# A ConvNeXt block and two Mamba layers in one kernel: convolution bands read with a sliding offset, six batches of convolution per stage, and a layer norm moved from VectorE to GpSimd

## The chip, the core and the metric

The kernel runs on one core of a Trainium2 chip. Its time is the device time of a whole execution in microseconds (us), shown as the median of several runs. A core has five engines that run their own instruction streams: TensorE (PE in the profile), VectorE (DVE), ScalarE (ACT), GpSimd (POOL) and SyncE (SP), which here issues nearly all DMAs.

## The reference, cut to what matters

Input is x of 32 x 96 x 56 x 56 in float32.

```python
# layer 0: ConvNeXt block
h = depthwise_conv7x7(x) + conv_b                  # padding 3, one 7x7 filter per channel
h = layernorm_over_channels(h) * ln_g + ln_b
x = (gelu(h @ w1 + b1) @ w2 + b2) * layer_scale + x
# layer 1: two Mamba blocks over the 3136 pixels as a sequence, then a fusion
for i in range(2):
    h = layernorm_over_channels(seq) * ln_g[i] + ln_b[i]
    xs, z = split(h @ in_w[i])                      # 2 x 192
    xc = silu(causal_conv4(xs));  dt, Bm, Cm = split(xc @ xproj_w[i])
    delta = softplus(dt @ dt_w[i] + dt_b[i])
    state = scan(exp(delta * A), delta * Bm * xc)   # 192 channels x 16 states
    y = sum_over_states(state * Cm) + Dp * xc
    seq = seq + (y * silu(z)) @ out_w[i]
out = batchnorm(fus_w @ concat(seq, relu(mean(x) @ gp_w)) + fus_b) + x
```

## The kernel before

**Prologue.** The depthwise convolution is done on TensorE, two channels at a time (48 pairs). The 112 rows of a pair's image (2 x 56) lie on the partitions. For each of the 7 column shifts dw, a 112 x 112 band matrix holds the 7 filter rows on its diagonals, and a matmul of `band[:, dw, :]` with the padded image shifted by dw adds into PSUM. `conv_pair` (L157 to L184) does this for the first `b0 = 12` batches: it builds the band in SBUF by seven `copy_predicated` operations on DVE (L165) with seven masks that GpSimd made, stores the band to DRAM (`band_d`, L170), runs 2 x 7 matmuls of 6 batches x 56 = 336 columns (L176), adds the bias on ACT (L180) and stores the result (`conv_d`, L184). Bands and padded images have three buffers each. A scheduler orders this part. Then the first block (layer 0 after the convolution) of batch 0 is done on its own: `block0`, whose reading of the convolution is `cv` (L408).

**Stages.** After that come 256 stages: for each batch and each quarter of its sequence (784 positions), one stage for each of the two Mamba layers. The order of all engines is written out by hand here: a stage has 24 steps (`NSTEP`; six groups j of 32 channels x four groups g of states), `run(n, slots)` emits every piece of other work whose slot is n, and a slot below 0 or above 23 lies in the stage before or after. A step is one scan on DVE (L959) over 785 elements. Its inputs:

- the decay, an exponential by ACT (`exps`, L905), into SBUF (`da`) or PSUM (`w`);
- the input term, u times B. For four of six j, PE spreads u over the states into PSUM (`spread`, L931, with some filler matmuls L917 ahead of it, `FILL`) and DVE multiplies by B (`times_b`, L887); for j = 2 and 5 (`POOLED`) GpSimd does it from a broadcast copy `us` (`pooled`, L941).

After every second scan GpSimd multiplies the states by C (L964), and PE adds them up into `y` (`add_up`, L1005). ACT copies the last states for the next quarter (`keep_state`, L973, `KS` steps after the scan). A state tile has 7 buffers.

Beside the scans, a stage holds these pieces:

- `prep` of the next stage: centring, squares and means of the layer norm on PE and ACT, `root` (L387, L388: ACT's Ln and Exp, in place in PSUM), then `norm`, two DVE multiplications of 96 x 392 (L611) into `hn`; projections (L625), silu, softplus, the product u = delta * xc on GpSimd (L707), and the loads of B, C, delta (`d4`) and `us`;
- `post` of the stage before: the output projection and its moves;
- in stages 2 to 249, `block0` of a half quarter (392 positions) of a later batch; its own norm on DVE is L435;
- in stages 2 to 193, `conv` of one pair for one group of `NB = 5` batches: it loads the band that the prologue stored (L542) and the image (L543), does 7 matmuls of 280 columns (L552), and stores `conv_d`.

**Final pass.** The statistics of the batch norm, then a pass over the output.

Of the kernel before, what the change touches and what calls it, by code (L numbers as in the profile page):

```python
# [34 lines left out]
F32 = mybir.dt.float32  # L35
I32 = mybir.dt.int32
AF = mybir.ActivationFunctionType
ALU = mybir.AluOpType
# [23 lines left out]
def convnext_mamba_kernel(  # L62
# [38 lines left out]
    NB = 5  # L101
    b0 = B - 4 * NB if B > 4 * NB else B
    groups = [(0, b0)] + [(b, b + NB) for b in range(b0, B, NB)]
# [4 lines left out]
    band_d = dram.tile([C // 2, 2 * H, 7 * 2 * H], F32, name="band_d")  # L108
# [12 lines left out]
    ones = cc.tile([R2, R2], F32, name="ones")  # L121
    nc.vector.memset(ones, 1.0)
    masks = []
    for dh in range(7):
        m = cc.tile([R2, R2], F32, name="m", tag="m", bufs=2)

        nc.gpsimd.affine_select(
            out=m, in_=ones, compare_op=ALU.is_equal, fill=0.0, base=3 - dh,
            pattern=[[-1, R2]], channel_multiplier=1,
        )  # L130
        nc.gpsimd.affine_select(
            out=m[:, 0:H], in_=m[:, 0:H], compare_op=ALU.is_ge, fill=0.0, base=H - 1,
            pattern=[[0, H]], channel_multiplier=-1,
        )
        nc.gpsimd.affine_select(
            out=m[:, H:R2], in_=m[:, H:R2], compare_op=ALU.is_ge, fill=0.0, base=-H,
            pattern=[[0, H]], channel_multiplier=1,
        )
        mi = cc.tile([R2, R2], I32, name=f"mi{dh}", tag=f"mi{dh}")
        nc.vector.tensor_copy(mi, m)  # L140
        masks.append(mi)
    cw = cc.tile([R2, C // 2, 49], F32, name="cw")
    wv = conv_w.rearrange("(p two) k -> two p k", two=2)
    bv = conv_b.rearrange("(p two) k -> two p k", two=2)
    for j in range(2):
        nc.sync.dma_start(cw[j * H : (j + 1) * H], wv[j].partition_broadcast(H))
        nc.sync.dma_start(
            cb[j * H : (j + 1) * H].unsqueeze(2), bv[j].partition_broadcast(H)
        )
    bands, xpads = [], []  # L150
    for i in range(3):
        t = cc.tile([R2, 7, R2], F32, name=f"band{i}", tag=f"band{i}")
        nc.gpsimd.memset(t, 0.0)
        bands.append(t)
        t = cc.tile([R2, b0, W + 6], F32, name=f"xpad{i}", tag=f"xpad{i}")
        nc.gpsimd.memset(t, 0.0)
        xpads.append(t)  # L157
    def conv_pair(p):
        xp, T = xpads[p % 3], bands[p % 3]
        nc.sync.dma_start(  # L160
            xp[:, :, 3 : 3 + W],
            x[0:b0, 2 * p : 2 * p + 2, :].rearrange("b c (h w) -> (c h) b w", w=W),
        )
        for dh in range(7):
            nc.vector.copy_predicated(  # L165
                T,
                masks[dh].unsqueeze(1).broadcast_to([R2, 7, R2]),
                cw[:, p, dh * 7 : (dh + 1) * 7].unsqueeze(2).broadcast_to([R2, 7, R2]),
            )
        nc.sync.dma_start(band_d[p], T.rearrange("p k n -> p (k n)"))  # L170
        ct = cx.tile([R2, b0 * W], F32, name="ct")
        for lo in range(0, b0, GB):
            n = min(GB, b0 - lo)
            ps = cps.tile([R2, GB * W], F32, name="ps")
            for dw in range(7):
                nc.tensor.matmul(  # L176
                    ps[:, 0 : n * W], T[:, dw, :], xp[:, lo : lo + n, dw : dw + W],
                    start=(dw == 0), stop=(dw == 6),
                )
            nc.scalar.activation(  # L180
                ct[:, lo * W : (lo + n) * W], ps[:, 0 : n * W], AF.Identity,
                bias=cb[:, p : p + 1],
            )
        nc.sync.dma_start(conv_d[0][p * R2 : (p + 1) * R2, :], ct)  # L184
# [161 lines left out]
    with ExitStack() as main:  # L346
# [12 lines left out]
        def tok(a):  # L359
            return slice(a * HC, (a + 1) * HC)  # L360
# [23 lines left out]
        def rsqrt(ps):  # L384

            rs = ps[0:C, 0:HC]
            nc.scalar.activation(rs, rs, AF.Ln, bias=eps_c[0:C])  # L387
            nc.scalar.activation(rs, rs, AF.Exp, scale=-0.5)  # L388
# [5 lines left out]

        batch_bias = {}
        batch_sums = {}

        def block0(b, c, s):
# [3 lines left out]
            def load():  # L402
                if k == 0:
                    batch_sums[b] = work([C, NCH * 2], "sums", 2)
                v["cv"] = work([C, ROWS, W], "cv", 1)
                g = 0 if b < b0 else 1 + (b - b0) // NB
                at = (b - groups[g][0]) * W
                nc.sync.dma_start(  # L408
                    v["cv"],
                    conv_d[g].rearrange("(c h) w -> c h w", h=H)[  # L410
                        :, k * ROWS : (k + 1) * ROWS, at : at + W
                    ],
                )
# [15 lines left out]
            def root():  # L429
                if pre and s == 0:  # L430
                    exp_ln_tables()
                rsqrt(v["ps"])

            def norm():
                nc.vector.tensor_tensor(hn0s[s][0:C], v["cv"], v["ps"][0:C, 0:HC], ALU.mult)  # L435
# [47 lines left out]
            def fuse():  # L483
# [12 lines left out]
                (-6, load), (2, load_x), (11.2, center), (11.9, square), (12.4, mean),  # L496
                (12.6, root), (14.1, True, norm), (15.6, up), (15.8, gelu), (17.3, down),
                (18, residual),
# [35 lines left out]
        nc.vector.memset(xpad, 0.0)  # L534

        def conv(g, p):
            lo, hi = groups[g]
            v = {}

            def load():  # L540
                v["band"] = wp.tile([R2, 7, R2], F32, name="band", tag="band", bufs=1)
                nc.sync.dma_start(v["band"].rearrange("p k n -> p (k n)"), band_d[p])  # L542
                nc.sync.dma_start(  # L543
                    xpad[:, :, 3 : 3 + W],
                    x[lo:hi, 2 * p : 2 * p + 2, :].rearrange("b c (h w) -> (c h) b w", w=W),
                )

            def tap(dw):
                def piece():
                    if dw == 0:  # L550
                        v["ps"] = psum(2)
                    nc.tensor.matmul(  # L552
                        v["ps"][0:R2, 0 : NB * W], v["band"][:, dw, :], xpad[:, :, dw : dw + W],
                        start=(dw == 0), stop=(dw == 6),
                    )

                return piece

            def store():
                t = wp.tile([R2, HC], F32, name="sq", tag="sq", bufs=3)[:, 0 : NB * W]  # L560
                nc.scalar.activation(
                    t, v["ps"][0:R2, 0 : NB * W], AF.Identity, bias=cb[:, p : p + 1]
                )
                nc.sync.dma_start(conv_d[g][p * R2 : (p + 1) * R2, :], t)

            at = (5.9, 6.1, 7.8, 8.6, 9.2, 9.6, 10.4)
            return [(-1, load), (10.5, store), *[(at[dw], tap(dw)) for dw in range(7)]]
# [3 lines left out]
        AHEAD = {(2, 0): 0, (2, 1): 4.4, (5, 0): 12.3, (5, 1): 16.9}  # L571
# [5 lines left out]
        def prep(S):  # L577
# [20 lines left out]
            def root():  # L598
                for a in range(2):
                    rsqrt(v["ps"][a])  # L600
# [5 lines left out]
            def norm(a):  # L606
                def piece():
                    hn = v["hn"] = hns[i]
                    if c == 0 and a == 0:
                        nc.vector.memset(hn[:, 0:3], 0.0)  # L610
                    nc.vector.tensor_tensor(  # L611
                        hn[0:C, 3 + a * HC : 3 + a * HC + HC], S.seq[:, tok(a)],
                        v["ps"][a][0:C, 0:HC], ALU.mult,
                    )

                return piece
# [113 lines left out]
            def load_d4(j):  # L730
# [10 lines left out]
                (-18, load), (-12.3, center), (-11.9, square), (-12.1, halo), (-11.6, mean),  # L741
                (-11.2, root), (-9, True, norm(0)), (-8.5, True, norm(1)),
            ]
            t = (-4.5, -4.4, -5.3, -4.8, -4, 0.2, 1.3, 2.3, 2.9, 3.4, 4)
            if S in (stages[2], stages[-1]):
# [3 lines left out]
                    (12, norm(0)), (12, norm(1)),  # L749
                ]  # L750
                t = (12, 12, 13, 13, 14, 14, 15, 16, 17, 18, 19)
            elif S is stages[3]:
# [3 lines left out]
                    (-3, root), (-2, norm(0)), (-2, norm(1)),  # L756
# [11 lines left out]
                (max(16.8, t[8] + 2.2), load_bc(1, 1)), (max(19.8, t[8] + 2.2), load_bc(0, 1)),  # L768
                (t[9], dt), (t[10], softplus),
                (max(14, t[10] + 1.5), product), (max(18.3, t[10] + 3.1), store_u(0)),  # L770
                (25.3, store_u(1)),
                (max(16.5, t[10] + 2), load_d4(0)), (max(21.9, t[10] + 3), load_d4(1)),
                (max(20.3, t[10] + 3.2), load_u(0)), (23, load_d4(2)),
                (26, load_d4(3)), (32.9, load_u(1)), (30, load_d4(4)), (34, load_d4(5)),
            ]

        def post(S):
# [55 lines left out]
            if i == 1:  # L833
                pieces += [(12.7, save), (17.2, stat(0)), (19, stat(1))]
# [8 lines left out]
        KS = 2  # L843
        FILL = {0: 4, 4: 12}
# [326 lines left out]
```

## Time and profile before

| | |
|---|---|
| median of 3 runs | 16063.91 us (16063.67 to 16070.08) |
| profiled execution | 16065.38 us, span 16063.7 us |
| mean granted TensorE clock | 0.931 |
| PE busy | 13868.6 us, 86% |
| DVE busy | 15341.8 us, 96% |
| ACT busy | 11941.9 us, 74% |
| POOL busy | 13950.6 us, 87% |
| DMA, mean rate | 147 GB/s |
| convolution of the prologue ends | 443 us |
| first and last product u (L707) | 541.49 us and 15635.07 us |

The span is the time from the first to the last instruction of the profiled execution; its own time is 1.7 us longer. Busy shares are averages over parts with different limits, so the prediction reads them by stretch. In a group of instructions, the first number after the bar is the busy time, the second the mean duration of one in ns, and behind the second bar stands the idle time of the engine just before them with what ended it. A row of L176, L552 or another fp32 matmul counts two records per matmul.

### The profile page before, as it was taken

How to read it: one execution, taken by the hardware profiler on the slowest of the kernel's cores; microseconds unless marked ns; L12 is line 12 of the kernel's file. 1: busy time of each engine (PE TensorE's matmuls, PEld its weight loads, DVE VectorE, ACT ScalarE, POOL GpSimd, SP SyncE). 2: the span in 40 equal slices, each digit the busy share in tenths (PEclk: the TensorE clock that was granted, in tenths of full speed). 3: DMA queues.
4: the chain of work that ended last, by engine and by line, in shares of the span. 5: the costliest groups of instructions: out<-in, count | busy, mean ns of one | idle time of the engine just before them, and what ended most of it. 6: DMA issues, size and time to landing. Idle time of an engine off the chain costs nothing. (4 is left out here: it accounts for less than half of the span.)

```text
span 16063.7 us, 215150 instructions
## 1 busy us (share of the span) xinstructions
PE 13868.6 (86%) x74840; PEld 5981.5 (37%) x74840; DVE 15341.8 (96%) x12358; ACT 11941.9 (74%) x23139; POOL 13950.6 (87%) x4446
## 2 busy tenths in 40 slices
PE   8888988888988888888898888889888888888870
PEld 5333333333333333333333333333333333333330
DVE  8699999999999999999999999999999999999993
ACT  1577777777777777777777777777777777777763
POOL 1599999999999999999999999999999999999980
PEclk9899999999999999999999999999999999999985
DMA  4344444444444444444444444444444444444438
GB/s 112 110 148 147 149 149 146 149 147 149 150 146 149 147 149 150 146 149 147 148 150 146 148 148 148 149 146 148 147 148 139 136 138 137 138 139 139 138 123 293
DMA packets 1307226, 2362.65 MB, mean 147 GB/s; under 512 B 495918, under 2 KB 697914, under 8 KB 1306136
## 3 DMA queue, kind: packets, MB, share of 16 engines
q1 hardware_dynamic: 1296808, 2308.46, 47.0%
q10 hardware_dynamic: 7168, 38.54, 0.6%
q8 instruction: 590, 9.67, 0.2%
q14 instruction: 500, 4.10, 0.1%
q0 software_dynamic: 2160, 1.88, 0.1%
HBM read 1945.97 MB, written 402.41 MB: 146 GB/s over the span
## 5 line engine op out<-in xcount | busy, mean ns | idle before, releaser
L964 POOL TENSOR_TENSOR h<-h,cp 128x1568 f32<-128x1568 f32 x3072 | 9968.7, 3249 | 1177.4 <-DVE h L959 974.4
L959 DVE TENSOR_TENSOR_SCAN h<-w,h 128x785 f32<-128x785 f32 (+1 forms) x3072 | 5293.9, 1769 | 122.9 <-ACT w L905 110.1
L959 DVE TENSOR_TENSOR_SCAN h<-da,w 128x785 f32<-128x785 f32 (+1 forms) x3072 | 5389.6, 1775 | 2.6 <-ACT da L905 2.6
L941 POOL TENSOR_TENSOR h<-us,bp 128x1570 f32<-128x1570 f32 x1024 | 3318.0, 3240 | 56.3 <-PE y L1005 29.8
L905 ACT ACTIVATE w<-d,A 128x784 f32<-128x784 f32 x3072 | 2819.1, 918 | 671.3 <-DVE h L959 587.7
L887 DVE TENSOR_TENSOR w<-w,bp 128x786 f32<-128x786 f32 x3072 | 2916.0, 980 | 146.4 <-PE w L931 24.7
L905 ACT ACTIVATE da<-d,A 128x784 f32<-128x784 f32 x3072 | 2876.5, 947 | 12.7 <-DMA d<-dd 11.9
L1005 PE MATMUL y<-h,ssum 128*32 128x392 f32 x24576 | 2460.1, 511 | 79.5 <-POOL h L964 79.2
L625 PE MATMUL ps<-hn,wx 97*64 97x392 f32 x12288 | 2204.2, 500 | 9.1 <-DVE hn L611 9.1
L931 PE MATMUL w<-u,sel 64*128 64x393 f32 x4096 | 998.0, 562 | 1328.2 <-DVE h L959 1233.2
L904 ACT COPY w<-st 128x1 f32<-128x1 f32 x2304 | 371.6, 161 | 1510.9 <-DVE h L959 1473.4
L625 PEld LDWEIGHTS ps<-hn,wx 97*64 97x64 f32 x12288 | 814.8, 136 | 1331.2 <-issue 1296.6
L1005 PEld LDWEIGHTS y<-h,ssum 128*32 128x32 f32 x24576 | 662.4, 111 | 1643.5 <-issue 1416.8
L552 PE MATMUL ps<-xpad,band 112*112 112x280 f32 x2688 | 1032.5, 509 | 259.3 <-ACT dl L695 259.3
L707 POOL TENSOR_TENSOR u<-dl,xc 128x1176 f32<-128x1176 f32 x256 | 685.6, 2678 | 489.2 <-ACT dl L695 470.7
L917 PEld LDWEIGHTS y<-sel 128*128 128x128 f32 x8192 | 981.6, 193 | 253.2 <-issue 184.1
L917 PE MATMUL y<-sel 128*128 128x120 f32 x8192 | 1029.3, 279 | 14.6 <-DVE z L980 14.6
L887 DVE TENSOR_TENSOR h<-w,bp 128x786 f32<-128x786 f32 x1024 | 990.1, 967 | 0.0
L367 ACT ACT_TABLE_LOAD x759 | 973.8, 1283 | 14.2 <-PEq L1158 0.8
L931 PEld LDWEIGHTS w<-u,sel 64*128 64x128 f32 x4096 | 331.5, 190 | 1716.5 <-DVE h L959 980.6
L552 PEld LDWEIGHTS ps<-xpad,band 112*112 112x112 f32 x2688 | 490.2, 207 | 871.2 <-issue 450.6
L792 PE MATMUL ps<-z,ow 64*96 64x392 f32 x3072 | 797.1, 668 | 0.0
(158 smaller groups left out, 15917.6 us busy)
## 6 DMA issues: line engine op xcount, KB each, us to landing
d<-dd SPq DMA_DIRECT2D x1536, 392.0 KB, 3.6
bp<-bd SPq DMA_DIRECT2D x1024, 392.0 KB, 4.6
cp<-bd SPq DMA_DIRECT2D x1024, 392.0 KB, 6.0
us<-uu SPq DMA_DIRECT2D x512, 392.0 KB, 4.5
dd<-dl SPq DMA_DIRECT2D x512, 294.0 KB, 3.7
band<-band_d SPq DMA_DIRECT2D x192, 343.0 KB, 5.8
uu<-u SPq DMA_DIRECT2D x1024, 49.0 KB, 3.4
cv<-conv_d SPq DMA_DIRECT2D x256, 147.0 KB, 2.7
```

The costliest lines, as they stand in the source:

```text
L367: nc.scalar.preload_act_table_set("natural_log_exp_and_others")
L552: nc.tensor.matmul(v["ps"][0:R2, 0 : NB * W], v["band"][:, dw, :], xpad[:, :, dw : dw + W], start=(dw == 0), stop=(dw == 6),)
L625: nc.tensor.matmul(v["x", q][rows(a), 0:HC], weights[:, k, 64 * q : 64 * q + 64], v["hn"][:, o : o + HC], start=(k == 0), stop=(k == last),)
L792: nc.tensor.matmul(v["ps"][a][0:C, 0:HC], S.d["ow"][rows(a), q, :], S.z[rows(a), q, :], start=False, stop=(q == NQ - 1),)
L887: nc.vector.tensor_tensor(halves(S.pb[j, g]), halves(S.u4[j])[:, :, 0 : HC + 1], halves(S.bc[0, g // 2][:, g % 2, :]), ALU.mult,)
L905: nc.scalar.activation(e[:, 1 : 1 + CH], S.d4[j], AF.Exp, scale=S.d["A"][:, j, g : g + 1])
L917: nc.tensor.matmul(spare, sel[:, 0, :], sel.rearrange("p a b -> p (a b)")[:, 0 : 512 - HC], start=True, stop=True,)
L931: nc.tensor.matmul(u4[:, 512 * a : 512 * a + HC + 1], sel[rows(a), j % 2, :], S.u[rows(a), j // 2, a : a + HC + 1], start=True, stop=True,)
L941: nc.gpsimd.tensor_tensor(states(S, j, h)[:, :, 0 : 1 + CH], S.us[j].unsqueeze(1).broadcast_to([128, 2, 1 + CH]), S.bc[0, h][:, :, 0 : 1 + ...
L959: nc.vector.tensor_tensor_scan(h[:, g % 2, at], S.e.pop((j, g))[:, at], S.pb.pop((j, g), h[:, g % 2, :])[:, at], 1.0 if c else 0.0, ALU.mu ...
L964: nc.gpsimd.tensor_tensor(h[:, :, 0:CH], h[:, :, 1 : 1 + CH], S.bc[1, g // 2], ALU.mult)
L1005: nc.tensor.matmul(S.y[r0 : r0 + 32, 0:HC], ssum, hs[k][:, g, tok(a)], start=False, stop=(half == 1 and g == 1),)
```

## The change

It has four parts that were made together.

1. The band is no longer built on the partitions. Each channel's 49 weights are laid out once as 7 rows of 112 with the seven filter rows in the middle (`bw`), and stored in DRAM (`band_d`, 96 x 7 x 112). `load_band` reads, for partition k, 56 values from offset k on: the offset slides by row. The band that results gives the image rows in reverse order, so `cv` is read back row by row, 7 DMAs in place of 1. Only the two diagonal 56 x 56 blocks are written; the rest of the band tile is set to zero once.
2. `NB` is 6 in place of 5, so the prologue convolves 8 batches (`b0`) in place of 12, in two groups of 4, and each of the 192 stage parts convolves 6.
3. The norm of the next stage is one GpSimd multiplication of 96 x 784 in place in `hn`, where ACT now writes the reciprocal root; the two DVE multiplications are gone. (`ZP = 0` leaves the norm of `block0` on DVE.)
4. `KS` goes from 2 to 1, `FILL` has one filler matmul less in each of its two places, and many slots are moved.

```diff
-    NB = 5
+    NB = 6
-    band_d = dram.tile([C // 2, 2 * H, 7 * 2 * H], F32, name="band_d")
+    band_d = dram.tile([C, 7, 2 * H], F32, name="band_d")
...
+    cw = cc.tile([C, 49], F32, name="cw")
+    nc.sync.dma_start(cw, conv_w)
+    bw = cc.tile([C, 7, R2], F32, name="bw")
+    nc.vector.memset(bw, 0.0)
+    nc.vector.tensor_copy(bw[:, :, H - 4 : H + 3], cw.rearrange("p (h w) -> p w h", w=7))
+    nc.sync.dma_start(band_d, bw)
     for j in range(2):
-        nc.sync.dma_start(cw[j * H : (j + 1) * H], wv[j].partition_broadcast(H))
         nc.sync.dma_start(
             cb[j * H : (j + 1) * H].unsqueeze(2), bv[j].partition_broadcast(H)
         )
+    def load_band(T, p):
+        for j in range(2):
+            w = band_d[2 * p + j]
+            r = slice(j * H, (j + 1) * H)
+            nc.sync.dma_start(
+                T[r, :, r], bass.AP(w.tensor, w.offset, [[1, H], [R2, 7], [1, H]])
+            )
...
-        for dh in range(7):
-            nc.vector.copy_predicated(...)
-        nc.sync.dma_start(band_d[p], T.rearrange("p k n -> p (k n)"))
+        load_band(T, p)
...
-        def rsqrt(ps):
+        def rsqrt(ps, out):
-            nc.scalar.activation(rs, rs, AF.Exp, scale=-0.5)
+            nc.scalar.activation(out, ln, AF.Exp, scale=-0.5)
...
-                nc.sync.dma_start(
-                    v["cv"],
-                    conv_d[g].rearrange("(c h) w -> c h w", h=H)[
-                        :, k * ROWS : (k + 1) * ROWS, at : at + W
-                    ],
-                )
+                rows_d = conv_d[g].rearrange("(c h) w -> c h w", h=H)
+                for r in range(ROWS):
+                    nc.sync.dma_start(
+                        v["cv"][:, r, :], rows_d[:, H - 1 - k * ROWS - r, at : at + W]
+                    )
...
-                v["band"] = wp.tile([R2, 7, R2], F32, name="band", tag="band", bufs=1)
-                nc.sync.dma_start(v["band"].rearrange("p k n -> p (k n)"), band_d[p])
+                load_band(band, p)
...
-            at = (5.9, 6.1, 7.8, 8.6, 9.2, 9.6, 10.4)
-            return [(-1, load), (10.5, store), *[(at[dw], tap(dw)) for dw in range(7)]]
+            at = (5.7, 5.9, 6.6, 8.7, 8.8, 9.4, 10.2)
+            return [(-1, load), (10.3, store), *[(at[dw], tap(dw)) for dw in range(7)]]
...
-            def norm(a):
-                def piece():
-                    hn = v["hn"] = hns[i]
...
-                    nc.vector.tensor_tensor(
-                        hn[0:C, 3 + a * HC : 3 + a * HC + HC], S.seq[:, tok(a)],
-                        v["ps"][a][0:C, 0:HC], ALU.mult,
-                    )
+            def norm():
+                hn = v["hn"]
+                if c == 0:
+                    nc.gpsimd.memset(hn[:, 0:3], 0.0)
+                hn = hn[0:C, 3 : 3 + CH]
+                nc.gpsimd.tensor_tensor(hn, S.seq, hn, ALU.mult)
...
-                (-11.2, root), (-9, True, norm(0)), (-8.5, True, norm(1)),
+                (-11.2, root), (-10, norm),
-            t = (-4.5, -4.4, -5.3, -4.8, -4, 0.2, 1.3, 2.3, 2.9, 3.4, 4)
+            t = (-4.5, -4.4, -5.8, -4.8, -4.1, -1.2, 1.3, 2.3, 2.9, 3.4, 4)
...
-                (max(16.8, t[8] + 2.2), load_bc(1, 1)), (max(19.8, t[8] + 2.2), load_bc(0, 1)),
+                (max(17.6, t[8] + 2.2), load_bc(1, 1)), (max(17.5, t[8] + 2.2), load_bc(0, 1)),
-                (max(14, t[10] + 1.5), product), (max(18.3, t[10] + 3.1), store_u(0)),
-                (25.3, store_u(1)),
-                (max(16.5, t[10] + 2), load_d4(0)), (max(21.9, t[10] + 3), load_d4(1)),
-                (max(20.3, t[10] + 3.2), load_u(0)), (23, load_d4(2)),
-                (26, load_d4(3)), (32.9, load_u(1)), (30, load_d4(4)), (34, load_d4(5)),
+                (max(14, t[10] + 1.5), product), (max(17.1, t[10] + 3.1), store_u(0)),
+                (27.4, store_u(1)),
+                (max(15.3, t[10] + 2), load_d4(0)), (max(21.9, t[10] + 3), load_d4(1)),
+                (max(20.3, t[10] + 3.2), load_u(0)), (22.3, load_d4(2)),
+                (29.1, load_d4(3)), (34.2, load_u(1)), (29.9, load_d4(4)), (34, load_d4(5)),
...
-        KS = 2
-        FILL = {0: 4, 4: 12}
+        KS = 1
+        FILL = {0: 3, 4: 11}
```

More of the change, by code (lines that the diff above doesn't have):

```diff
@@ L98, in convnext_mamba_kernel @@
     const = ctx.enter_context(tc.tile_pool(name="const", bufs=1))
-    NB = 5
+    NB = 6
     b0 = B - 4 * NB if B > 4 * NB else B
-    groups = [(0, b0)] + [(b, b + NB) for b in range(b0, B, NB)]
+    groups = [(0, b0)] + [(b, min(b + NB, B)) for b in range(b0, B, NB)]
     conv_d = [
@@ L120, in convnext_mamba_kernel @@
     cps = first_conv.enter_context(tc.tile_pool(name="cp", bufs=6, space=PSUM))
-    ones = cc.tile([R2, R2], F32, name="ones")
-    nc.vector.memset(ones, 1.0)
-    masks = []
-    for dh in range(7):
[L125 to L129, printed above, removed]
-        )
-        nc.gpsimd.affine_select(
-            out=m[:, 0:H], in_=m[:, 0:H], compare_op=ALU.is_ge, fill=0.0, base=H - 1,
-            pattern=[[0, H]], channel_multiplier=-1,
-        )
[L135 to L143, printed above, removed]
+    cw = cc.tile([C, 49], F32, name="cw")
[4 more added lines that the diff above has]
+    nc.sync.dma_start(band_d, bw)
     bv = conv_b.rearrange("(p two) k -> two p k", two=2)
     for j in range(2):
-        nc.sync.dma_start(cw[j * H : (j + 1) * H], wv[j].partition_broadcast(H))
         nc.sync.dma_start(
@@ L152, in convnext_mamba_kernel @@
         t = cc.tile([R2, 7, R2], F32, name=f"band{i}", tag=f"band{i}")
-        nc.gpsimd.memset(t, 0.0)
+        nc.vector.memset(t, 0.0)
         bands.append(t)
@@ L163, in conv_pair @@
         )
[L164 to L169, printed above, removed]
-        nc.sync.dma_start(band_d[p], T.rearrange("p k n -> p (k n)"))
+        load_band(T, p)
         ct = cx.tile([R2, b0 * W], F32, name="ct")
@@ L382, in mean_of @@
             return ps
-        def rsqrt(ps):
-            rs = ps[0:C, 0:HC]
-            nc.scalar.activation(rs, rs, AF.Ln, bias=eps_c[0:C])
-            nc.scalar.activation(rs, rs, AF.Exp, scale=-0.5)
+        def rsqrt(ps, out):
+            ln = ps[0:C, 0:HC]
+            nc.scalar.activation(ln, ln, AF.Ln, bias=eps_c[0:C])
+            nc.scalar.activation(out, ln, AF.Exp, scale=-0.5)
+        ZP = 0
         batch_bias = {}
@@ L407, in load @@
                 at = (b - groups[g][0]) * W
-                nc.sync.dma_start(
-                    v["cv"],
-                    conv_d[g].rearrange("(c h) w -> c h w", h=H)[
-                        :, k * ROWS : (k + 1) * ROWS, at : at + W
-                    ],
-                )
+                rows_d = conv_d[g].rearrange("(c h) w -> c h w", h=H)
[3 more added lines that the diff above has]
+                    )
             def load_x():
@@ L431, in root @@
                     exp_ln_tables()
-                rsqrt(v["ps"])
+                v["rs"] = hn0s[s][0:C] if ZP else v["ps"][0:C, 0:HC]
+                rsqrt(v["ps"], v["rs"])
             def norm():
-                nc.vector.tensor_tensor(hn0s[s][0:C], v["cv"], v["ps"][0:C, 0:HC], ALU.mult)
+                eng = nc.gpsimd if ZP and not pre else nc.vector
+                eng.tensor_tensor(hn0s[s][0:C], v["cv"], v["rs"], ALU.mult)
             def up():
@@ L495, in block0 @@
             return last + [
-                (-6, load), (2, load_x), (11.2, center), (11.9, square), (12.4, mean),
-                (12.6, root), (14.1, True, norm), (15.6, up), (15.8, gelu), (17.3, down),
-                (18, residual),
+                (-6, load), (2, load_x), (11.2, center), (12, square), (12.4, mean),
+                (12.6, root), ((14.1, norm) if ZP else (14.1, True, norm)), (15, up), (15.2, gelu), (17.3, down),
+                (17.7, residual),
             ]
@@ L534, in convnext_mamba_kernel @@
         nc.vector.memset(xpad, 0.0)
+        band = wp.tile([R2, 7, R2], F32, name="band", tag="band", bufs=1)
+        nc.vector.memset(band, 0.0)
         def conv(g, p):
             lo, hi = groups[g]
+            nb = hi - lo
             v = {}
             def load():
-                v["band"] = wp.tile([R2, 7, R2], F32, name="band", tag="band", bufs=1)
-                nc.sync.dma_start(v["band"].rearrange("p k n -> p (k n)"), band_d[p])
+                load_band(band, p)
                 nc.sync.dma_start(
-                    xpad[:, :, 3 : 3 + W],
+                    xpad[:, 0:nb, 3 : 3 + W],
                     x[lo:hi, 2 * p : 2 * p + 2, :].rearrange("b c (h w) -> (c h) b w", w=W),
@@ L552, in piece @@
                     nc.tensor.matmul(
-                        v["ps"][0:R2, 0 : NB * W], v["band"][:, dw, :], xpad[:, :, dw : dw + W],
+                        v["ps"][0:R2, 0 : nb * W], band[:, dw, :], xpad[:, 0:nb, dw : dw + W],
                         start=(dw == 0), stop=(dw == 6),
@@ L559, in store @@
             def store():
-                t = wp.tile([R2, HC], F32, name="sq", tag="sq", bufs=3)[:, 0 : NB * W]
+                t = wp.tile([R2, HC], F32, name="sq", tag="sq", bufs=3)[:, 0 : nb * W]
                 nc.scalar.activation(
-                    t, v["ps"][0:R2, 0 : NB * W], AF.Identity, bias=cb[:, p : p + 1]
+                    t, v["ps"][0:R2, 0 : nb * W], AF.Identity, bias=cb[:, p : p + 1]
                 )
                 nc.sync.dma_start(conv_d[g][p * R2 : (p + 1) * R2, :], t)
-            at = (5.9, 6.1, 7.8, 8.6, 9.2, 9.6, 10.4)
-            return [(-1, load), (10.5, store), *[(at[dw], tap(dw)) for dw in range(7)]]
+            at = (5.7, 5.9, 6.6, 8.7, 8.8, 9.4, 10.2)
+            return [(-1, load), (10.3, store), *[(at[dw], tap(dw)) for dw in range(7)]]
         POOLED = (2, 5)
-        AHEAD = {(2, 0): 0, (2, 1): 4.4, (5, 0): 12.3, (5, 1): 16.9}
+        AHEAD = {(2, 0): 0.6, (2, 1): 4.4, (5, 0): 12.3, (5, 1): 16.9}
         seqs = {}
@@ L598, in root @@
             def root():
+                v["hn"] = hns[i]
                 for a in range(2):
-                    rsqrt(v["ps"][a])
+                    rsqrt(v["ps"][a], hns[i][0:C, 3 + a * HC : 3 + a * HC + HC])
             def halo():
@@ L604, in halo @@
                     nc.scalar.copy(hns[i][:, 0:3], hns[i][:, CH : CH + 3])
-            def norm(a):
-                def piece():
-                    hn = v["hn"] = hns[i]
-                    if c == 0 and a == 0:
-                        nc.vector.memset(hn[:, 0:3], 0.0)
-                    nc.vector.tensor_tensor(
-                        hn[0:C, 3 + a * HC : 3 + a * HC + HC], S.seq[:, tok(a)],
-                        v["ps"][a][0:C, 0:HC], ALU.mult,
-                    )
-                return piece
+            def norm():
[4 more added lines that the diff above has]
+                nc.gpsimd.tensor_tensor(hn, S.seq, hn, ALU.mult)
             def project(q, weights, taps_, first, last):
@@ L740, in prep @@
             start = [
-                (-18, load), (-12.3, center), (-11.9, square), (-12.1, halo), (-11.6, mean),
-                (-11.2, root), (-9, True, norm(0)), (-8.5, True, norm(1)),
+                (-18, load), (-12.3, center), (-12, square), (-12.1, halo), (-11.6, mean),
+                (-11.2, root), (-10, norm),
             ]
-            t = (-4.5, -4.4, -5.3, -4.8, -4, 0.2, 1.3, 2.3, 2.9, 3.4, 4)
+            t = (-4.5, -4.4, -5.8, -4.8, -4.1, -1.2, 1.3, 2.3, 2.9, 3.4, 4)
             if S in (stages[2], stages[-1]):
@@ L748, in prep @@
                     (10.3, center), (10.4, square), (10.5, halo), (10.9, mean), (11, root),
-                    (12, norm(0)), (12, norm(1)),
+                    (12, norm),
                 ]
@@ L755, in prep @@
                     (-18, load), (-4.5, center), (-4.4, square), (-4.3, halo), (-3.5, mean),
-                    (-3, root), (-2, norm(0)), (-2, norm(1)),
+                    (-3, root), (-2, norm),
                 ]
@@ L833, in post @@
             if i == 1:
-                pieces += [(12.7, save), (17.2, stat(0)), (19, stat(1))]
+                pieces += [(12.7, save), (17.2, stat(0)), (18.7, stat(1))]
             return pieces
```

## The prediction

> **What bounds the kernel now.** I read the busy times by stretch first, because this run has four parts: the prologue's convolution (0 to 443 us), the first block of batch 0 (to 541), 256 stages (to about 15,635) and the final pass. Columns: stretch, length, then busy us and instructions of PE, PEld, DVE, ACT, POOL, the granted clock, the DMA share, GB/s.
>
> ```profile
> 48.00:443.00 395.00, 390.59 (x1367) 238.50 (x1365) 336.72 (x355) 51.47 (x97) 20.76 (x36) 0.99 0.44 117
> 541.00:15635.00 15094.00, 13356.96 (x73024) 5688.09 (x73022) 14792.49 (x11815) 11692.61 (x22807) 13846.76 (x4333) 0.94 0.47 145
> ```
>
> In the first stretch PE is busy 390.6 of 395 us: TensorE binds, DVE (337) stands close behind. In the second DVE is busy 14,792 of 15,094 us, 98%; POOL has 92%. The costliest groups of the page, and two groups from the answer by line, say what fills them:
>
> ```profile
> L964 POOL TENSOR_TENSOR h<-h,cp 128x1568 f32<-128x1568 f32 x3072 | 9968.7, 3249 | 1177.4 <-DVE h L959 974.4
> ...
> L959 DVE TENSOR_TENSOR_SCAN h<-da,w 128x785 f32<-128x785 f32 (+1 forms) x3072 | 5389.6, 1775 | 2.6 <-ACT da L905 2.6
> ...
> L887 DVE TENSOR_TENSOR w<-w,bp 128x786 f32<-128x786 f32 x3072 | 2916.0, 980 | 146.4 <-PE w L931 24.7
> ```
>
> ```profile
> L165 DVE COPY_PREDICATED band<-mi,cw 112x784 f32<-112x784 int32 x336 | 346.9, 1037 | 32.1 <-PE ps L176 20.3 <-DMA cw<-in_conv_w 2.9
> ...
> L611 DVE TENSOR_TENSOR hn<-seq,ps 96x392 f32<-96x392 f32 x512 | 258.6, 544 | 36.4 <-ACT ps L388 36.4
> ```
>
> DVE's scans wait for almost nothing. The timeline of one stage shows the norm that moves (L611) between two scans, with no gap around it, and POOL at the same moment:
>
> ```profile
> 8049.76 1.78 DVE L959 TENSOR_TENSOR_SCAN h<-da,w 128x785 f32<-128x785 f32 x1
> 8051.46 0.53 DVE L435 TENSOR_TENSOR hz<-cv,ps 96x392 f32<-96x392 f32 x1
> 8051.91 1.77 DVE L959 TENSOR_TENSOR_SCAN h<-da,w 128x785 f32<-128x785 f32 x1
> 8053.61 1.00 DVE L611 TENSOR_TENSOR hn<-seq,ps 96x392 f32<-96x392 f32 x2
> 8054.54 1.77 DVE L959 TENSOR_TENSOR_SCAN h<-w,h 128x785 f32<-128x785 f32 x1
> ```
>
> ```profile
> 8051.62 3.24 POOL L964 TENSOR_TENSOR h<-h,cp 128x1568 f32<-128x1568 f32 x1 [1.05 <-DVE h L959]
> 8054.85 2.67 POOL L707 TENSOR_TENSOR u<-dl,xc 128x1176 f32<-128x1176 f32 x1
> 8057.48 3.26 POOL L964 TENSOR_TENSOR h<-h,cp 128x1568 f32<-128x1568 f32 x1
> ```
>
> L707 runs once a stage, so its starts give the period: of 243 stages from the fifth on, 145 take 58.0 to 58.7 us (a stage in which DVE never stops), 67 take 59.6 or more, the mean is 59.02. The 0.56 us above 58.46 is stalls. The waits between 4000 and 12000 us (135 stages) name them: 61.6 us of ACT's exponentials coming late, and POOL's reserve beside it, 512 us or 3.8 a stage.
>
> ```profile
> DVE h L959 <- ACT w L905: 61.6, 45, 2.0
> ```
>
> ```profile
> POOL h L964 <- DVE h L959: 512.2, 679, 2.2
> ```
>
> [...] the trace has 3249/1568 = 2.07. [...] L964 between 4000 and 12000 us took 3.22 to 3.31 us under a DVE that is 98% busy[...].
>
> **The change part by part.**
>
> *Norm off DVE.* The pair of L611 takes 0.93 us from start to next start (8053.61 to 8054.54). Out of a stage without gaps that is 58.46 to 57.53. In 254 stages: **-236 us**. In two stages (the third and the last), norm and projections follow at once; there it waits on POOL behind a 3.25 us product, about +4 each: **+8**.
>
> *Norm on POOL.* One operation of 784 elements: by rate 784 x 2.07 = 1.62 us; by the line through L964 and L707 (1.46 ns an element and 0.96 us fixed) 2.1. I take 1.8. POOL has 54.4 us of work a stage (12 x 3.25, 4 x 3.2, 2.63), so 56.2 against 57.5: covered by its wait for scans. It stands behind L707 and ahead of the product of scan 15. That product ends at about 8062.6 instead of 8060.7; PE's sums that read it came at 8004.78 + 58.4 = 8063.2 in the stage's rhythm. The next thing behind them on PE, the spread of u for the next stage, waits 1.34 us for DVE already. So nothing, with 0.5 to 1.9 us of cover. If the cover is gone, the spread is late next, then L887.
>
> *Exponentials into SBUF, keep_state one step earlier (KS), other slots.* ACT's write target changes, not its count. At the steps with the tightest exchange, the ACT exponential waits for the same scan that the earlier state copy needs; elsewhere ACT's lead shrinks by a step. Not shown before; between -0.56 (all stalls gone) and +0.6 us a stage; I take 0.
>
> *Conv of 6 batches in 192 stages.* Seven matmuls go from 280 to 336 columns; at 1.70 ns a column (0.57 us for 336 in the prologue) that is +0.67 us of PE a stage, less two filler matmuls (L917, about 0.28 together): +0.4. PE's idle time is 6.8 us a stage (15,094 less 13,357, over 255). Hidden; the next spread (wait 0.80) would be late if not.
>
> *Transfers of a stage.* SP issues 7 instead of 1 for cv and 2 instead of 1 for band; at 0.36 and 0.59 us each (SP timeline at 8007 to 8014) +2.8 us. The results are wanted some 17 steps, 40 us, later. Moved ahead of cv's issue are store_u(0), load_bc and load_d4(0); load_u(1) now stands behind load_d4(5), so us lands at about 32 us of the stage while POOL wants it at 31.5 and has until 36. The band becomes 784 runs of 224 bytes for 112 of 3136; cv, 672 such runs, lands in 2.7 us. DMA share is 47%. I take 0; bound 0 to +0.5.
>
> *Prologue.* The 336 L165 operations go, but PE bound. A pair takes 7.98 us (ACT's L180 two by two); 14 matmuls of 224 columns take 14 x 0.38 = 5.32. 48 pairs: **-128**. DMA per pair: 1680 short runs; 1344 of them landed in 4.4 us before. Three buffers give a band load about 10.6 us from release to need, for some 7 of issue and landing: hidden. At the start, SP's queue shows what delays the first matmul (47.8 us):
>
> ```profile
> 0.81 0.45 SPq L146 DMA_DIRECT2D cw<-in_conv_w  x1
> 1.31 2.13 SPq L147 DMA_DIRECT2D cb<-in_conv_b  x1
> 3.50 11.82 SPq L146 DMA_DIRECT2D cw<-in_conv_w  x1
> 15.36 10.17 SPq L147 DMA_DIRECT2D cb<-in_conv_b  x1
> 25.57 20.85 SPq L160 DMA_DIRECT2D xpad<-in_x  x3
> ```
>
> The broadcasts of cw go; two of cb stay (some 10 us each), then a band_d write and the first band load, each 3 to 4 us: first matmul at 31 (bounds 15 and 45): **-17**. The first block waits for 6 more issues in front of its first cv and some of its second: **+5**; its following norm on POOL **+1**.
>
> Sum: -236 + 8 - 128 - 17 + 5 + 1 = -367. The profiled execution took 16065.4 us, 1.5 above the median: 15,698, or **15,697** against the median.
>
> **The rivals.** (1) *The remaining ACT stalls go too*, because several ACT pieces get new slots: 254 x 0.56 = 142 less, 15,555. For it: 145 stages already run free. Against: the pieces that collide with the pooled scans (moves at 8.9 and 9.2) stay. (2) *The prologue becomes bound by band loads.* If a pair stays at 8 us, 128 are lost: 15,825. For it: each load now waits for a released buffer and stands in SP behind a ct store; against: 10.6 us of lead. (3) *POOL's lateness reaches DVE*, slower than before: norm puts POOL at 98% of DVE's period; once the product of scan 15, or a pooled product that waits for us, is over 1.9 us late, PE's sums hold back the next spread and DVE stands. At 2 us a stage it gives +508: 16,205. It decides from 367/254 = 1.44 us a stage. For it: covers of 0.5 to 1.9 us. Against: POOL needs to grow by 1.3 + 1.4 us a stage beyond my 1.8, a norm of 4.5. (4) *The change does not do what it says*: the built program's instruction order has L611's successor on POOL behind u, and none of it on DVE. Not likely.
>
> **How the numbers follow.** The likeliest case 0.60, rival 1 0.13, rival 2 0.11, rival 3 0.13, no net change by a mixture 0.03. The range goes from rival 1 less 15 us (an earlier first matmul), 15,540, to rival 2 plus 0.4 us of stalls a stage, 15,920. Faster 0.84, within 0.2% (32 us, about what a measurement of this kernel tells from no change) 0.03, slower 0.13.
>
> **What would show it.** Right: L176's successor at about 5.3 us a pair and the stages starting near 400; starts of the u product 57.5 apart in most stages; the norm at 1.6 to 2.1 us on POOL; POOL's wait for DVE down to about 1.3 us a stage. Wrong: waits of L887 for PE's spread, of PE's y for POOL, of h L941 for us, or of scans for ACT's w above 1 us a stage; PE waiting for band in the prologue.

## The result and the profile after

The changed kernel takes **16,568.8 us** (median of 4 runs, 16,568.4 to 16,586.5) against 16,064.5 before: a ratio of 1.032, 95% interval 1.030 to 1.033. It is 504 us slower; 367 us faster was forecast. The profiled execution is the highest of the four, 16,586.5 us, 18 above the median.

The starts of the product u on GpSimd (L707 before, L694 now) divide the difference between the two profiled executions, +521 us:

| part | before | after | difference |
|---|---|---|---|
| up to the first u | 541.5 | 410.3 | -131 |
| first to last u (255 periods) | 15,093.6 | 15,740.8 | +647 |
| after the last u | 428.6 | 433.7 | +5 |

So the prologue gave nearly what it was to give (139 us were forecast), and the stages lost 2.5 us each: the mean period is 61.6 us in stages with a convolution and 61.5 in those without, where it was 59.0. The profile of the same window as before, 541 to 15,635 us, in the same columns (the stages of the kernel after run from 410 to 16,151, so the whole window lies within them):

```profile
541.00:15635.00 15094.00, 13554.89 (x69472) 5577.47 (x69469) 14055.50 (x10808) 11268.96 (x22005) 13704.30 (x4469) 0.94 0.46 138
```

DVE, 98% busy before, is 93% busy; PE stands at 90% and POOL at 91%. By busy time alone no engine is full. What each waits for says more. In these answers, for 4000 to 12000 us or 130 stages, the numbers behind the colon are the us in total, the number of waits and the longest one:

```profile
PEld y L992 <- POOL h L951: 581.6, 437, 1.9
POOL h L928 <- DMA us<-uu: 488.3, 101, 5.7
...
ACT z L625 <- PE ps L612: 388.3, 390, 2.7
...
DVE h L946 <- ACT w L892: 304.7, 251, 2.5
...
DVE z L967 <- PE y L992: 171.6, 130, 1.6
...
POOL h L951 <- DVE h L946: 77.8, 260, 2.7
```

GpSimd's old reserve, waiting for DVE, is 0.6 us a stage (3.8 before). In its place stands a wait for the load of `us`: 101 stages name the DMA, 4.8 us each, and the 29 others name an instruction that ended near the same moment (626 us together over 130 stages, again 4.8 each). Work of 56.0 us (7,276 busy over 130), 4.8 and 0.6 make 61.4: **the period is GpSimd's**. One stage on GpSimd:

```profile
8116.62 6.54 POOL L951 TENSOR_TENSOR h<-h,cp 128x1568 f32<-128x1568 f32 x2 [0.20 <-DVE h L946]
8123.35 6.65 POOL L951 TENSOR_TENSOR h<-h,cp 128x1568 f32<-128x1568 f32 x2 [0.19 <-DVE h L946]
8134.39 3.23 POOL L928 TENSOR_TENSOR h<-us,bp 128x1570 f32<-128x1570 f32 x1 [4.38 <-DMA us<-uu]
8137.58 3.24 POOL L951 TENSOR_TENSOR h<-h,cp 128x1568 f32<-128x1568 f32 x1
8140.78 2.69 POOL L694 TENSOR_TENSOR u<-dl,xc 128x1176 f32<-128x1176 f32 x1
8143.43 1.84 POOL L603 TENSOR_TENSOR hn<-seq,hn 96x784 f32<-96x784 f32 x1
8145.23 3.25 POOL L951 TENSOR_TENSOR h<-h,cp 128x1568 f32<-128x1568 f32 x1
```

The gap of 4.38 us stands ahead of the pooled product of j = 5; from there on GpSimd runs without a pause into the next stage. The queue of SP at that time:

```profile
8115.04 9.85 SPq L721 DMA_DIRECT2D d<-dd  x3
8124.98 1.20 SPq L663 DMA_DIRECT2D bp<-bd  x2
8126.28 1.20 SPq L663 DMA_DIRECT2D cp<-bd  x2
8127.57 0.56 SPq L710 DMA_DIRECT2D us<-uu  x1
```

Slot 34.2 of one stage and slots 10 and 10.2 of the next are the same place, so load_u(1) is issued behind the sixth load of delta *and* the four broadcasts of B and C for the stage to come. us is issued at 8127.57 and arrives at about 8134.3, where GpSimd's wait ends, some 6.7 us later; in the kernel before this second load of us took 4.3 (median of 128), and it stood ahead of all five (8035.69 against 8041.77 to 8044.87).

How GpSimd's lateness reaches DVE is seen some 30 us earlier, behind the late pooled product of the stage before, in one line each of PE, ACT and DVE:

```profile
8100.46 1.51 PE L992 MATMUL y<-h,ssum 128*32 128x392 f32 x12 [1.09 <-POOL h L951]
```

```profile
8102.83 0.50 ACT L625 ACTIVATE z<-ps 128x392 f32<-128x392 f32 x1 [2.66 <-PE ps L612]
```

```profile
8107.11 1.79 DVE L946 TENSOR_TENSOR_SCAN h<-w,h 128x785 f32<-128x785 f32 x1 [1.70 <-ACT w L892]
```

PE's sums wait for GpSimd's product; the projection of z behind them on PE's queue is late; ACT waits for it with silu of z; the exponential behind that is late; DVE's scan waits, 2.3 us a stage in all (304.7 over 130). DVE's own product with y (L967) waits for the late sums directly, another 1.3.

### The profile page after: what moved, and what is told of

Read it like the earlier page. It is cut to its first block, busy times and chain, and to the rows that moved or that the text cites. A ratio compares the mean times of both kernels' runs of the same rounds, so it can differ in the third digit from the quotient of the medians.

```text
span 16584.8 us, 215686 instructions
## 1 busy us (share of the span) xinstructions
PE 14442.4 (87%) x73816; PEld 6060.2 (37%) x73816; DVE 14833.0 (89%) x11444; ACT 11923.2 (72%) x23139; POOL 14364.8 (87%) x4742
## 4 chain that ended last, share of the span: by engine, by line
POOL 27%; PE 20%; DVE 16%; DMA 12%; ACT 12%; issue 11%; SPq 2%; POOLq 0%; DVEq 0%; ACTq 0%
POOL h L951 20%; DVE h L946 13%; PE y L992 5%; DMA us<-uu 4%; PE ps L612 4%; POOL h L928 3%; PE ps L543 3%; DMA cp<-bd 3%; ACT da L892 3%; POOL hn L603 2%; DMA d<-dd 2%; ACT L354 2%; ACT w L892 2%; DVE w L874 2%; PE ps L163 2%
## 5 line engine op out<-in xcount | busy, mean ns | idle before, releaser
L992 PE MATMUL y<-h,ssum 128*32 128x392 f32 x24576 | 3035.5, 514 | 597.8 <-POOL h L951 594.4
L992 PEld LDWEIGHTS y<-h,ssum 128*32 128x32 f32 x24576 | 746.8, 110 | 2649.6 <-issue 1413.2
L543 PE MATMUL ps<-xpad,band 112*112 112x336 f32 x2688 | 1296.8, 612 | 237.2 <-ACT dl L682 237.2
L904 PEld LDWEIGHTS y<-sel 128*128 128x128 f32 x7168 | 863.6, 192 | 247.0 <-issue 182.4
L625 ACT ACTIVATE z<-ps 128x392 f32<-128x392 f32 x768 | 381.9, 497 | 753.5 <-PE ps L612 753.2
L674 PE MATMUL ps<-dbl,dtw 6*64 6x392 f32 x3072 | 733.5, 537 | 213.2 <-ACT dbl L647 213.2
L904 PE MATMUL y<-sel 128*128 128x120 f32 x7168 | 911.0, 279 | 7.7 <-DVE z L967 7.7
L543 PEld LDWEIGHTS ps<-xpad,band 112*112 112x112 f32 x2688 | 540.6, 227 | 964.0 <-issue 522.9
L603 POOL TENSOR_TENSOR hn<-seq,hn 96x784 f32<-96x784 f32 x256 | 471.9, 1843 | 323.7 <-ACT hn L375 317.0
```

What stands on the lines that cost most here:

```text
L543: nc.tensor.matmul(v["ps"][0:R2, 0 : nb * W], band[:, dw, :], xpad[:, 0:nb, dw : dw + W], start=(dw == 0), stop=(dw == 6),)
L603: nc.gpsimd.tensor_tensor(hn, S.seq, hn, ALU.mult)
L904: nc.tensor.matmul(spare, sel[:, 0, :], sel.rearrange("p a b -> p (a b)")[:, 0 : 512 - HC], start=True, stop=True,)
L992: nc.tensor.matmul(S.y[r0 : r0 + 32, 0:HC], ssum, hs[k][:, g, tok(a)], start=False, stop=(half == 1 and g == 1),)
```

## Experiments

Three theories were open. A: the place of load_u(1) in SP's queue makes GpSimd stand. B: GpSimd's norm alone does it. C: the short runs of the new loads slow all transfers. Kernels 1, 3 and 4 and the kernel after put the norm and that slot each in both places; kernel 2 moves the slot alone in the kernel before. Each ratio is against the kernel before, timed beside the kernel in question.

**1. After, with us early.**

```diff
-                (29.1, load_d4(3)), (34.2, load_u(1)), (29.9, load_d4(4)), (34, load_d4(5)),
+                (29.1, load_d4(3)), (32.9, load_u(1)), (29.9, load_d4(4)), (34, load_d4(5)),
```

> The kernel after, with one slot put back: the second load of us, load_u(1), at 32.9 as before in place of 34.2, so that SP issues it ahead of the sixth load of delta and of the loads of B and C. Theory A (the place of that load in SP's queue makes GpSimd stand, and with the norm GpSimd has no reserve left): GpSimd's wait for us goes from 3.6 us a stage to under 0.5, the period from 61.5 to 57.5 to 58.3 us, the time to 15,600 to 15,850. Theory B (the norm on GpSimd alone, through PE's sums that come late): a period of 61 us or more, 16,450 to 16,570. Theory C (short runs of the bands and seven-fold cv loads slow all transfers): us still lands 2 us or more late, 16,100 to 16,400.

Measured: 15,774.8 us, ratio 0.982 (0.981 to 0.984). The wait for us is gone from GpSimd's list; the fastest stages take 57.47 us, the mean is 58.4. SP issues us ahead of the sixth load of delta, 11 us before GpSimd wants it:

```profile
8124.44 0.51 SPq L710 DMA_DIRECT2D us<-uu  x1
8129.83 0.51 SPq L721 DMA_DIRECT2D d<-dd  x1
```

GpSimd at the same place:

```profile
8128.80 6.65 POOL L951 TENSOR_TENSOR h<-h,cp 128x1568 f32<-128x1568 f32 x2 [0.20 <-DVE h L946]
8135.40 3.24 POOL L928 TENSOR_TENSOR h<-us,bp 128x1570 f32<-128x1570 f32 x1
8139.68 3.23 POOL L951 TENSOR_TENSOR h<-h,cp 128x1568 f32<-128x1568 f32 x1 [1.03 <-DVE h L946]
8142.90 2.68 POOL L694 TENSOR_TENSOR u<-dl,xc 128x1176 f32<-128x1176 f32 x1
8145.53 1.85 POOL L603 TENSOR_TENSOR hn<-seq,hn 96x784 f32<-96x784 f32 x1
```

The pooled product starts without a gap, and GpSimd catches up with DVE ahead of u. One moved DMA issue is worth 794 us. Theory A holds; B and C fall as causes of the loss, since norm, band loads and cv loads are all still there.

**2. Before, with us late.**

```diff
-                (26, load_d4(3)), (32.9, load_u(1)), (30, load_d4(4)), (34, load_d4(5)),
+                (26, load_d4(3)), (34.2, load_u(1)), (30, load_d4(4)), (34, load_d4(5)),
```

> The kernel before, with the same slot alone moved the other way: load_u(1) at 34.2 in place of 32.9. Theory A: GpSimd waits some 3 to 4.5 us a stage for us; its reserve of 3.8 us takes most of that, so 16,050 to 16,300, likeliest 16,190, with a wait of h L941 for us above 2 us a stage. Theories B and C: nothing changes, within 0.2% of 16,064.

Measured: 16,357.8 us, ratio 1.019 (1.017 to 1.021). Direction and cause are as expected (the first row is GpSimd's wait, from the answer by waits); the size is above the range by 58 us. The wait ahead of that product is 4.9 us a stage (104 of 133 stages name the load), more than the 3 to 4.5 expected; GpSimd's wait for DVE, its reserve, falls from 3.8 us a stage to 0.9.

```profile
POOL h L941 <- DMA us<-uu: 510.3, 104, 6.3
POOL h L964 <- DVE h L959: 124.2, 280, 2.3
```

The slot alone makes the kernel before slower, with none of the other parts.

**3. After, with the norm on DVE and us late.** The norm is as in the kernel before:

```diff
-                    rsqrt(v["ps"][a], hns[i][0:C, 3 + a * HC : 3 + a * HC + HC])
+                    rsqrt(v["ps"][a], v["ps"][a][0:C, 0:HC])
...
-                (-11.2, root), (-10, norm),
+                (-11.2, root), (-9, True, norm(0)), (-8.5, True, norm(1)),
...
```

> The kernel after with the norm back on DVE as in the kernel before (root in PSUM, two multiplications on DVE between the same scans), load_u(1) left at 34.2. Theory A: GpSimd keeps its wait of 4.6 us for us but has 1.84 us less work, so the period is 59.4 to 59.9 us: 16,020 to 16,150. Theory B: the stages run as before, 59.0 us, and the shorter prologue remains: 15,930. Theory C: 60 us or more, above 16,170.

Measured: 16,166.4 us, ratio 1.007 (1.005 to 1.008), 16 us above A's range. GpSimd's wait for us is still there, 483 us in the 99 of 133 stages that name the load:

```profile
POOL h L932 <- DMA us<-uu: 483.1, 99, 6.5
```

**4. After, with both put back.** Experiment 3 with load_u(1) at 32.9.

> The kernel after with both put back: norm on DVE and load_u(1) at 32.9. What remains of the change is the band reading, the six batches per stage, KS, FILL and the other slots. Theories A and B: a period of 58.5 to 59.1 us, 15,800 to 15,950. Theory C: 59.5 us or more, above 16,050.

Measured: 15,974.9 us, ratio 0.995 (0.993 to 0.996), 25 us above the range. The fastest stages with a convolution take 58.41 us, as in the kernel before; the mean is 59.3.

The four together, medians in us:

| | us early (32.9) | us late (34.2) | cost of late |
|---|---|---|---|
| norm on DVE (3, 4) | 15,975 | 16,166 | +191 |
| norm on GpSimd (1, after) | 15,775 | 16,569 | +794 |
| gain of the move | -200 | +402 | |

The two parts do not simply add. The wait ahead of the pooled product is 4.8 to 4.9 us a stage in all three kernels with us late (after, 2 and 3), whether the norm is on GpSimd or not. What differs is GpSimd's work, 54.1 us a stage in experiment 3 and 56.0 in the kernel after. With us early the norm's move gains 200 us; with us late, 4.8 us of wait and 1.84 us of norm are in series on one engine, and the same move loses 402.

**5. us behind the load of delta, ahead of the broadcasts.**

```diff
-                (29.1, load_d4(3)), (34.2, load_u(1)), (29.9, load_d4(4)), (34, load_d4(5)),
+                (29.1, load_d4(3)), (29.9, load_d4(4)), (34, load_d4(5)), (34, load_u(1)),
```

> The kernel after with load_u(1) issued directly behind the sixth load of delta, but ahead of the four broadcasts of B and C that slot 34.2 puts it behind (slot 34, last of its entries). It tells apart what of the lateness of us comes from which neighbour. Theory A1 (the four broadcasts: 2.6 us of issue[...]): us lands at about 29 us of the stage, in time for GpSimd; wait for us under 1 us a stage, 15,750 to 15,900. Theory A2 (SP standing at the sixth load of delta until ACT frees its buffer): two thirds of the wait stay, above 2.5 us a stage, 16,150 to 16,450.

Measured: 15,779.5 us, ratio 0.982 (0.980 to 0.983), the same as experiment 1. SP's queue and GpSimd's wait:

```profile
8126.91 0.51 SPq L721 DMA_DIRECT2D d<-dd  x1
8127.53 0.54 SPq L710 DMA_DIRECT2D us<-uu  x1
8128.12 1.24 SPq L663 DMA_DIRECT2D bp<-bd  x2
```

```profile
POOL h L928 <- DMA us<-uu: 6.9, 16, 0.8
```

Here the pooled product started at 8132.48 without a gap, so us had landed within 5.0 us. From the issue of us to the moment when GpSimd is free for that product there are 11.6 us in experiment 1, 5.0 here and 2.4 in the kernel after (medians of 4000 to 12000 us). So the place behind the load of delta costs no time, but it takes 6.6 us of the lead and leaves just enough. The four broadcasts take 2.6 more for their issue, and us lands later behind them: in experiment 2, whose trace shows the landings, 7.0 us after its issue (median of 131) where the kernel before has 4.3. The broadcasts have to stand ahead of us for the wait to arise. Whether they would do it without the delay behind delta, and whether their issue or the slower landing alone would be enough, was not tried.

**6 to 8. The remaining stalls.** Experiment 1 has 0.9 us of stalls a stage above its fastest, 57.47, against 0.6 above 58.41 in the kernel before.

```diff
# 6: experiment 1 with
-        KS = 1
+        KS = 2
# 7: experiment 1 with the compute slots of before
-                (-6, load), (2, load_x), (11.2, center), (12, square), (12.4, mean),
-                (12.6, root), ((14.1, norm) if ZP else (14.1, True, norm)), (15, up), (15.2, gelu), (17.3, down),
-                (17.7, residual),
+                (-6, load), (2, load_x), (11.2, center), (11.9, square), (12.4, mean),
+                (12.6, root), ((14.1, norm) if ZP else (14.1, True, norm)), (15.6, up), (15.8, gelu), (17.3, down),
+                (18, residual),
...
-                (-18, load), (-12.3, center), (-12, square), (-12.1, halo), (-11.6, mean),
+                (-18, load), (-12.3, center), (-11.9, square), (-12.1, halo), (-11.6, mean),
...
-            t = (-4.5, -4.4, -5.8, -4.8, -4.1, -1.2, 1.3, 2.3, 2.9, 3.4, 4)
+            t = (-4.5, -4.4, -5.3, -4.8, -4, 0.2, 1.3, 2.3, 2.9, 3.4, 4)
...
-                pieces += [(12.7, save), (17.2, stat(0)), (18.7, stat(1))]
+                pieces += [(12.7, save), (17.2, stat(0)), (19, stat(1))]
# 8: 6 and 7 together
```

> The kernel after with load_u(1) at 32.9 and KS back at 2. In the first of these two alone the stages still stand 0.9 us each for ACT's exponentials, against 0.56 in the kernel before. If KS = 1 is what shortens ACT's lead: stalls back to 0.5 to 0.6 us a stage, 15,670 to 15,720. If not: within 0.2% of 15,775.

> The kernel after with load_u(1) at 32.9 and the slots of the compute pieces as in the kernel before (block0's square, up, gelu and residual; stat(1); the next stage's square and six projections); the loads, the conv taps and KS stay as changed. If these slots cause the additional ACT stalls: 15,670 to 15,720. If not: within 0.2% of 15,775; slower is possible, since the projections then stand closer behind GpSimd's norm.

> Both edits of the last two kernels together. If KS and the slots only work together, it is faster than either; if neither matters, 15,775 within 0.2%; if both do, 15,650 to 15,700.

Measured: 6 takes 15,763.6 us (ratio 0.981, 0.980 to 0.983), 7 takes **15,713.5** (0.978, 0.976 to 0.979), 8 takes 15,742.3 (0.980, 0.978 to 0.981). KS = 2 gains nothing that these runs can tell: 11 us less than experiment 1 with overlapping executions, and with the compute slots of before 29 us more than experiment 7, where the executions do not overlap but the intervals of the ratios do. The compute slots of before are worth 61 us. DVE waits less for ACT: 100.5 us in experiment 1, 40.8 in experiment 7, both in 4000 to 12000 us. In the whole run that wait falls by 104 us (183.4 to 79.7); a part is lost elsewhere, 12 us of it ahead of the first u (424 against 412).

```profile
DVE h L946 <- ACT w L892: 40.8, 50, 1.7
```

The stage's mean is 58.1 us, the stalls are 0.6. Experiment 7 beats both kernels, the kernel before by 356 us (16,069.5 beside it). Which of its slots does it was not tried apart.

## Why the prediction was wrong

**The step that failed is "Transfers of a stage".** It read the queue correctly up to one item: "load_u(1) now stands behind load_d4(5), so us lands at about 32 us of the stage while POOL wants it at 31.5 and has until 36". The stage above starts at 8096.6 (DVE's first product with B): GpSimd was ready at 33.4 us, and us arrived at 37.7. The four broadcasts (slots 10 and 10.2) that stand between load_d4(5) and slot 34.2 were not counted. Experiment 5 shows that with them behind us the place behind load_d4(5) costs nothing; with them ahead, "I take 0; bound 0 to +0.5" became a wait of 4.8 us a stage. "Has until 36" failed as well: it is 4.5 us of cover, where the prediction's own sum leaves GpSimd 1.3 (57.5 less 56.2).

**The cover was counted twice.** The norm adds 1.84 us to GpSimd's work and shortens DVE's stage (without gaps 58.41 us in experiment 4, 57.47 in experiment 1), so it uses up most of the reserve that was to cover a late us. With the norm on DVE, GpSimd's work and the wait for us make 54.1 + 4.8 = 58.9 us, near the 59.3 that a stage takes with us early (experiment 4). With the norm on GpSimd they make 56.0 + 4.8 = 60.8, against 58.4 (experiment 1). That is why the same slot costs 191 us with the norm on DVE and 794 with it on GpSimd.

**Rival 3 was the right mechanism**, "a pooled product that waits for us", with too small a price: 2 us a stage over the forecast, where it is 61.5 less 57.5, and less the stalls of the forecast, 3.4. Its way to DVE was half right: PE's sums are late, but the next spread hardly is (DVE waits 1.9 us for it in all 130 stages); the projection of z behind the sums and ACT's silu carry the delay, and DVE's own wait for y.

The other steps, by their own numbers:

- *Norm off DVE*: 57.53 us for a stage without gaps was worked out, 57.47 and 57.48 stand in experiments 1 and 7. The whole gain of the move, with us early, is 200 us against 228 (236 less 8).
- *Norm on POOL*: 1.8 us taken, 1.84 measured, between the rate of the trace (1.62) and the line through the two rows (2.1).
- *Prologue*: 5.32 us a pair taken; ACT's L167 shows 5.34 (median). First u 131 us earlier against 139 forecast (-128 - 17 + 5 + 1), because the first matmul came at 47.0 us, outside my 15 to 45 (47.8 before: 1 us gained, not 17); the pairs themselves gave 131, from 390 us between the first and last L180 to 259 between those of L167. I took some 10 us for each broadcast of cb, though my own lines show 2.13 and 10.17, and left the image load behind them out. The two of cb, 10.8 us of SP, and the first image, 22.9 more, kept the band's store back until 35:

```profile
1.20 10.83 SPq L129 DMA_DIRECT2D cb<-in_conv_b  x2
12.07 22.87 SPq L153 DMA_DIRECT2D xpad<-in_x  x1
34.98 2.76 SPq L126 DMA_DIRECT2D band_d<-bw  x1
```

- *Two exposed stages*, +8: in experiment 1 they take 82.7 and 81.0 us, before 81.6 and 81.8. Nothing of +4 each is seen.
- *Conv of 6 batches* and the short runs: with the norm on DVE and us early (experiment 4) a stage without gaps takes 58.41, as before. Hidden, as taken, though PE's part was sized too small: its convolution in experiment 1 is busy 1.2 us a stage longer than before (+0.67 taken), the filler 0.46 less (0.28 taken).
- *KS*: 0 taken, no gain seen from putting it back. *Other slots*: 0 taken; the compute slots cost 61 us.

With the load put back, the kernel takes 15,775 us where 15,697 was forecast, and 15,713 with the compute slots of before.

## What to carry to other kernels

SP's queue issued in the built order here: us at 8127.57 us after the broadcasts from 8124.98 in the kernel after, us at 8127.53 ahead of those from 8128.12 in experiment 5. When a load moves in such a queue, list every transfer that then stands between it and its release, from the built order, and slots that wrap into the next stage too. Here the neighbour that was moved past on purpose only used up the lead (11.6 us to 5.0), and with the four broadcasts ahead of it too, the load came late (4.8 us of wait a stage). Two changes that draw on the same reserve of an engine, here 1.84 us of norm and 4.8 of wait against 3.8, have to be summed on that engine before either is costed at nothing. GpSimd at 91% was the bound here: its work of 56.0 us and the waits of 4.8 and 0.6 make 61.4 of a period of 61.5.

## What the runs showed of the hardware that I had not expected

The second broadcast load of us, 392 KB, took 4.3 us from issue to landing in the kernel before (median of 128) and 7.0 in experiment 2 (median of 131), directly behind four others of 392 KB each. In the kernel after, two loads of cb, 10.5 KB each, held SP for 10.8 us, and the image load behind them for another 22.9 us, in which time the queue moved 3,292 packets of 4 bytes each; of the other image loads of the prologue the next two took 2.4 us of SP together and the rest 0.32 each. What slowed that first one was not tried. GpSimd's product of 96 x 784 took 1.84 us (median of 130, 1.83 to 1.87) beside a DVE that is 93% busy. With it, the 128 x 1568 product took 3.25 us as before, and DVE's scans 1.77 and 1.78 as before (medians of 4000 to 12000 us).
